# Batched matrix square roots in lanes: far sets in 29 rounds instead of 27, with reads back from DRAM, statistics loads and input loads moved in their queues

## The chip, the cores and the metric

The kernel runs on one core of a Trainium2 chip. A core has engines with an instruction queue each, which run in order: TensorE (PE; its weight loads are shown as PEld), VectorE (DVE), ScalarE (ACT), GpSimd (POOL) and SyncE (SP), which here only issues DMAs. They wait for each other through semaphores. DMAs are issued from SyncE's and ScalarE's queues and carried by 16 DMA engines. The metric is the device time of one execution in microseconds, lower is better. Before the change it is 2986.16 us, the median of three runs (2984.56 to 2987.19).

## The reference

The input `x` has 32 batches of 32 channels of 128x128 matrices, in float32. Two layers add to it:

```python
def _L0_conv_ref(A):                       # 1024 matrices, 128x128
    normA = jnp.sqrt(jnp.sum(A2 * A2, axis=(1, 2)))
    Y = A2 / normA[:, None, None]; Z = I
    for _ in range(5):                     # Newton-Schulz, matrix square root
        T = 0.5 * (3.0 * I - jnp.matmul(Z, Y))
        Y = jnp.matmul(Y, T)
        Z = jnp.matmul(T, Z)
    return Y * jnp.sqrt(normA)[:, None, None]

x = x + _L0_conv_ref(_gn(x))               # _gn: group norm, 16 groups of 2 channels
x = x + _L1_conv_ref(_gn(x), weights1, weights2)
```

`_L1_conv_ref` takes the real part of a 2-D Fourier transform, multiplies 32x32 low modes (two corners) by real weights over the channels, and takes the real part of the inverse transform.

## The kernel before, in words

**Sets.** Four channels of one batch are a set, so there are 32 x 8 = 256 sets. The square root of a set is a fixed chain of products on TensorE: each product is four matmuls of 128x128, one for each channel, into one PSUM bank. Between two products VectorE or ScalarE takes the result out of PSUM, scaled and added to something. The generator `newton` (line 462) is the chain of one set; at each `yield` it hands over to the next set. `rest` stands for two yields.

**Lanes and rounds.** The main loop (lines 1115 to 1154) has nine lanes. In a round every lane that holds a set takes one step, up to the next `yield`. A set in a lane therefore advances by one step a round, and between two of its steps lie those of the other lanes. All engines' orders are exactly the order in which the steps issue their instructions (`keep_in_program_order`, line 88); no scheduler moves them. A new set starts when a lane is free and `due` is reached, which grows by `FAR` or `NEAR` rounds for each set (line 42).

**Near and far sets.** Both need a matrix `m` and its transpose `mb`. A near set (batch 0 and batches 19 to 31, 112 sets) transposes on TensorE (`near_quartic`, line 407). A far set (batches 1 to 18, 144 sets) transposes through DRAM: VectorE transposes 32x32 blocks out of PSUM (`turned`), a DMA writes them to DRAM (`away`, tile `turn`), and a second DMA reads them back in another order (`back`, tiles `w` and `mb`). There are three such round trips in a far set: one `w` in each of two `far_quartic` calls (line 442), and one `mb` in `newton` (line 481). The `far_quartic` of the second call takes `v` (a tile named `r`) that GpSimd makes from `mb` just before (line 486). In a far set 27 steps lie between start and end, and one starts every 27/9 = 3 rounds.

**Round-trip positions, before.** In `far_quartic` the way out follows the first product; the way back is issued two rounds later, and the product that uses `w` three rounds after that. `mb` goes back two rounds after its way out; its use by GpSimd follows four rounds later, in the same round as the next product.

**Inputs.** `fetch` (line 366) loads `b` and `xt` of a set, the latter transposed, three sets ahead of the lane's start: far sets on SyncE's queue, near sets on ScalarE's. `staged` (line 375) normalises them on ScalarE and GpSimd. `prep` (line 222) computes the group statistics of two batches at a time from a third copy `xs`, loaded on ScalarE's queue three steps ahead of the two `bn_stats` on VectorE that read it; all of the first loads are issued in its first step.

**After the square root.** `settle` (line 521) writes the sum to DRAM (`mid`), folds it on GpSimd for the Fourier transform and takes statistics on VectorE. `wide_products`, `small_products`, `last_products` and `inverse` (lines 670 to 1029) do the second layer; they run beside the near sets of batches 19 to 31, in steps that the main loop hands out by the round number. `weights` (line 848) loads weights of the last group into tiles that are free by then.

**Buffers.** Tiles come in rings. `rooms` (line 308) gives for each name the size of its ring and of a second part that exists until the end of the first 158 sets. DRAM tiles `turn` have a ring of 12. DMAs use eight completion semaphores in turn, so one is issued only when the one eight before it has landed.

Of the kernel before, what the change touches and what calls it, by code (L numbers as in the profile page):

```python
# [38 lines left out]
C = 32  # L39
G = 16  # L40
LANES, LESS = 9, 5
FAR, NEAR = 27 / 9, 25 / 5
GROUPS = (20, 7, 3, 2)


# [48 lines left out]
def conv_preact_kernel(  # L94
# [49 lines left out]
        od.append(dram.tile(shape, F32, name=f"od{i}", tag=f"od{i}"))  # L144
    where = [(i, b) for i, n in enumerate(GROUPS) for b in range(n)]

    stp = ctx.enter_context(tc.tile_pool(name="stp", bufs=4))
    up = ctx.enter_context(tc.tile_pool(name="up", bufs=1))
    sp = ctx.enter_context(tc.tile_pool(name="sp", bufs=1))
    small = ctx.enter_context(tc.tile_pool(name="small", bufs=1))  # L150
# [71 lines left out]
    def prep(bs, made):  # L222

        n = len(bs)
        nc_, ng = n * C, n * G
        first_b = bs[0]
        st = small.tile([P, ng, 6], F32, tag="a_st", name=f"a_st{first_b}", bufs=2)
        tiles = []
        parts = [(b, i) for b in bs for i in range(C // 4)]

        ahead = 3 if first_b else 8

        def load(k):
            b, i = parts[k]
            if first_b or i < 4:
                t = stp.tile([P, 2, 2 * P], F32, tag="xs", name=f"xs{b}_{i}")
            else:
                t = four("turn", True).rearrange("p (j c) x -> p j (c x)", j=2)
            src = xs_in[b, :, 2 * i : 2 * i + 2].rearrange("p g h c -> p g (h c)")
            kept(nc.scalar.dma_start(out=t, in_=src))  # L240
            tiles.append(t)

        for k in range(ahead):
            load(k)
        yield
        for k in range(len(parts)):
            for j in range(2):
                nc.vector.bn_stats(st[:, 2 * k + j, :], tiles[k][:, j, :])
            yield
            if k + ahead < len(parts):  # L250
                load(k + ahead)
        ms = small.tile([P, ng], F32, tag="a_ms", name=f"a_ms{first_b}")
        nm, d = yield from moments(st, ms, "a")
        yield from pause
        pq = bank()[:, 0, 0:nc_]
        nc.tensor.matmul(pq, avg_mean, d.rearrange("p g c -> p (g c)"), start=True, stop=True)
        if not first_b:
            warm(5)

        v = small.tile([P, nc_ + ng], F32, tag="a_v", name=f"a_v{first_b}")  # L260
        nc.vector.tensor_scalar_mul(v[:, 0:nc_], pq, -512 / (P * P))
        yield
        vg = small.tile([P, ng], F32, tag="a_vg", name=f"a_vg{first_b}")
        nc.vector.tensor_reduce(
            vg, v[:, 0:nc_].rearrange("p (g c) -> p g c", c=2), AX.X, ALU.add
        )
        nc.vector.tensor_scalar(v[:, nc_:], vg, 0.5, EPS, ALU.mult, ALU.add)
        yield
        s = small.tile([P, nc_ + ng], F32, tag="a_r_s", name=f"a_r_s{first_b}", bufs=2)
        yield from root(v, nc_ + ng, s)  # L270
        iv = small.tile([P, nc_ + ng], F32, tag="a_inv", name=f"a_inv{first_b}")
        nc.vector.reciprocal(iv, s)
        yield

        sc = small.tile([P, nc_], F32, tag="a_sc", name=f"a_sc{first_b}", bufs=2)
        nc.vector.tensor_scalar_mul(sc, iv[:, 0:nc_], MS / P)
        off = small.tile([P, ng, 2], F32, tag="a_off", name=f"a_off{first_b}", bufs=2)
        nc.vector.tensor_tensor(
            off,
            sc.rearrange("p (g c) -> p g c", c=2),  # L280
            nm[:, :, None].to_broadcast([P, ng, 2]),
            ALU.mult,
        )
        off = off.rearrange("p g c -> p (g c)")
        sn = small.tile([P, nc_], F32, tag="a_t_s", name=f"a_t_s{first_b}", bufs=3)
        for k, b in enumerate(bs):
            g, c = slice(k * G, k * G + G), slice(k * C, k * C + C)
            made[b] = (nm[:, g], sc[:, c], off[:, c], sn[:, c])
        yield
        nn = small.tile([P, ng, 2], F32, tag="a_d", name=f"a_n{first_b}")  # L290
        nc.vector.tensor_tensor(
            nn,
            s[:, 0:nc_].rearrange("p (g c) -> p g c", c=2),
            iv[:, nc_:, None].to_broadcast([P, ng, 2]),
            ALU.mult,
        )
        nn = nn.rearrange("p g c -> p (g c)")
        for far in sorted({is_far(b) for b in bs}):
            of = [k for k, b in enumerate(bs) if is_far(b) == far]
            c = slice(of[0] * C, of[-1] * C + C)  # L300
            f = EYE_Q * QS if far else EYE * QF
            nc.vector.tensor_scalar_mul(nn[:, c], nn[:, c], P * (1.5 / f) ** 2)
        yield
        yield from root(nn, nc_, sn)
        yield


    rooms = dict(b=(4, 6), xt=(10, 5), x=(3, 2), r=(4, 0), v=(3, 2), w=(3, 2), q=(4, 2))
    rooms.update(my=(4, 3), mb=(2, 4), t=(3, 2), y4=(2, 2), turn=(0, 4))
    turns = dict.fromkeys(rooms, 0)  # L310

# [28 lines left out]
    def minus(eye, m, t):  # L340

        nc.gpsimd.tensor_tensor(t, eye, m, ALU.subtract)
        return t
# [13 lines left out]
    def is_far(b):  # L357
        return 0 < b < FIRST
# [5 lines left out]
    raw = {}  # L364

    def fetch(b, g):
        queue = nc.sync if is_far(b) else nc.scalar
        xt, t = four("xt", has_more(b, g)), four("b", has_more(b, g))
        kept(queue.dma_start(out=t, in_=x[b, :, 4 * g : 4 * g + 4, :]))
        kept(queue.dma_start(out=xt, in_=xt_in[b, :, 4 * g : 4 * g + 4, :]))  # L370
        raw[b, g] = xt, t
# [35 lines left out]
    def near_quartic(m, mb, more):  # L407


        v = plus(m, -QA * MS, products(mb, m), "v", more)  # L410
        yield
        r = four("r", more)
        nc.gpsimd.tensor_tensor(r, mb, eye, ALU.add)
        yield
        w = plus(transposed(v), 1.0, r, "w", more)
        yield from rest
        q = plus(products(v, w), QF / (16 * MS**4), eye, "q", more)
        yield from rest
        return q
# [22 lines left out]
    def far_quartic(m, mb, v, f, later, more):  # L442

        ps = products(m, mb)
        held = away(turned(ps, more))
        if later:
            yield
        nc.vector.scalar_tensor_tensor(v, ps, 1 / (9 * MS), v, ALU.mult, ALU.add)
        if not later:
            yield  # L450
        minus(eye_q, m, m)
        yield
        w = back(held, "w", more)
        yield
        yield from rest
        q = plus(products(v, by_rows(w)), 9 / (39 * MS**2 * f**2), m, "q", more)
        yield from rest
        return q
# [3 lines left out]
    def newton(g, sn, xt, m, mb, v, far, more):  # L462
# [13 lines left out]
        if far:  # L476
            held = away(turned(ps, more))
            yield
            nc.scalar.mul(m, ps, MS / qf)
            yield  # L480
            mb = back(held, "mb", more)
            yield from rest
            yield from rest
            v = four("r", more)
            form = "p c (a j) -> p c a j"
            minus(eye_p.rearrange(form, a=4), by_rows(mb), v.rearrange(form, a=4))
            q = yield from far_quartic(m, by_rows(mb), v, TURNED, True, more)
            w, y4 = four("t", more), four("y4", more)
            nc.scalar.mul(w, products(q, by_rows(mb)), 1 / (MS * qf * TURNED))
            ps = products(q, y)  # L490
            for j in range(4):
                c = 4 * g + j
                nc.scalar.mul(y4[:, j, :], ps[:, j, :], sn[:, c : c + 1])
        else:
            nc.scalar.mul(m, ps, MS / qf)
            yield from rest
            mb = taken(transposed(m), "mb", more)
            yield from rest
            q = yield from near_quartic(m, mb, more)
            both = [bank().rearrange("p (j k) x -> p j k x", k=2) for _ in range(2)]  # L500
            for j in range(4):
                nc.tensor.matmul(both[j // 2][:, j % 2], q[:, j], my[:, j], start=True, stop=True)
            w, y4 = four("t", more), four("y4", more)
            for h in range(2):
                nc.scalar.mul(w[:, 2 * h : 2 * h + 2, :], both[h][:, :, 1, :], 1 / (MS * qf))
            for j in range(4):
                c = 4 * g + j
                nc.scalar.mul(y4[:, j, :], both[j // 2][:, j % 2, 0, :], sn[:, c : c + 1])
# [339 lines left out]
    def weights():  # L848


        kinds = [("b", 2)] * 3 + [("x", 2), ("b", 4), ("x", 4), ("x", 10)]
        kinds += [("my", 11)] * 2 + [("r", 12)] * 3 + [("mb", 15)] * 2 + [("v", 15)] * 2
        kinds += [("w", 16)] * 2 + [("my", 16), ("r", 17), ("v", 18)] + [("q", 19)] * 3
        first = B * C // 4 - 10
        spare = []
        for half in range(4, 2 * KK):
# [367 lines left out]
```

## Time and profile before

| what | value |
|---|---|
| median of three runs | 2986.16 us |
| profiled execution | 2981.79 us |
| its span, first to last instruction | 2980.0 us |
| TensorE busy (matmul) | 2849.7 us |
| VectorE busy | 2285.7 us |
| ScalarE busy | 1541.3 us |
| GpSimd busy | 1988.4 us |
| mean granted TensorE clock | 0.988 |
| bytes moved by DMA | 711.90 MB |

The page lists busy time, shares over time, DMA queues, the chain of work that ended last and the costliest groups of instructions. Views of the trace show more: who waited for whom (the engine and the tile it writes, the releaser, us in total, times, longest), the busy time of each engine in chosen stretches, the instructions of one tile, and instructions in order of time, where the number in brackets is the idle time before one and what ended it. A name such as `w<-turn` says what an instruction writes and reads; all instructions carry line 88, the recording helper's, so tiles and not lines tell them apart. A float32 matmul shows as two passes, so one product of four matmuls shows as eight.

### The profile page before, as it was taken

Reading aid. Unit: us, or ns where it says so; the run is one execution under the profiler, and the core shown is the slowest. Engines: PE = TensorE matmul, PEld = TensorE weight load, DVE = VectorE, ACT = ScalarE, POOL = GpSimd, SP = SyncE. Lnnn points to the kernel's source line nnn. Section 1 sums busy time; section 2 is a strip of 40 time slices with the busy share of each in tenths; the row PEclk is TensorE's granted clock in tenths of the full one; section 3 lists DMA queues with packets and bytes.
Section 4 is the critical chain, followed back from the end, with each engine's and each line's share of the span. In section 5 each row is a group of like instructions: output and inputs, shape, how many; then the busy total and the mean of one; then the engine's idle time right before and its main releaser. Section 6 shows DMA issues by size and latency. Waiting matters only on the chain.

```text
span 2980.0 us, 73661 instructions
## 1 busy us (share of the span) xinstructions
PE 2849.7 (96%) x27688; PEld 2663.8 (89%) x27688; DVE 2285.7 (77%) x4407; ACT 1541.3 (52%) x3899; POOL 1988.4 (67%) x2308
## 2 busy tenths in 40 slices
PE   7999999999999999999999999999999999999995
PEld 7899999999999899999999888888888899888983
DVE  7878898889788888888876545886876876777665
ACT  4555555555555555555544445545555544655452
POOL 4667767777777767767755534777777763678452
PEclk9999999999999999999999999999999999999997
DMA  5688889888888889898943566867877737666567
GB/s 177 199 280 272 253 267 281 275 266 282 269 275 257 283 253 294 253 291 255 303 139 104 157 203 208 284 231 242 281 242 248 261 124 226 209 230 218 186 211 268
DMA packets 566897, 711.90 MB, mean 239 GB/s; under 512 B 94736, under 2 KB 329232, under 8 KB 566544
## 3 DMA queue, kind: packets, MB, share of 16 engines
q1 hardware_dynamic: 494400, 574.26, 59.9%
q10 hardware_dynamic: 72144, 132.94, 13.7%
q8 instruction: 221, 3.62, 0.5%
q14 instruction: 132, 1.08, 0.1%
HBM read 440.17 MB, written 266.86 MB: 237 GB/s over the span
## 4 chain that ended last, share of the span: by engine, by line
PE 72%; DMA 12%; DVE 9%; issue 2%; POOL 2%; ACT 1%; SPq 1%; ACTq 0%; DVEq 0%; POOLq 0%
PE ps L88 72%; DMA xs<-in_xs 3%; DMA w<-turn 3%; DVE yt L88 1%; DVE turn L88 1%; DMA turn<-turn 1%; DVE b_d L88 1%; DMA yt<-mid 1%; DMA ob<-od 1%; DVE a_st L88 1%; DVE root L88 1%; DVE q L88 1%; DVE b_st L88 1%; SPq L88 1%; DVE v L88 1%
## 5 line engine op out<-in xcount | busy, mean ns | idle before, releaser
L88 POOL TENSOR_TENSOR fold<-xt 128x256 f32<-128x256 f32 x512 | 364.1, 734 | 308.4 <-DVE xt L88 274.2
L88 ACT ACTIVATE b<-b,a_off,a_sc 128x128 f32<-128x128 f32 x1024 | 467.2, 492 | 127.2 <-issue 27.9
L88 ACT ACTIVATE my<-ps 128x512 f32<-128x512 f32 x512 | 302.4, 602 | 410.4 <-PE ps L88 278.0
L88 PE MATMUL ps<-my,q 128*128 128x128 f32 (+1 forms) x2944 | 475.9, 309 | 6.5 <-ACT my L88 6.4
L88 POOL TENSOR_TENSOR yt<-yt,d 128x512 f32<-128x512 f32 x244 | 306.6, 1283 | 212.3 <-ACT d L88 192.8
L88 PEld LDWEIGHTS ps<-my,q 128*128 128x128 f32 x2944 | 411.9, 191 | 35.4 <-ACT my L88 7.6
L88 PE MATMUL ps<-w,v 128*128 128x128 f32 x2944 | 399.2, 279 | 26.1 <-DMA w<-turn 11.9
L88 POOL TENSOR_TENSOR v<-eye_v,b 128x512 f32<-128x512 f32 x144 | 184.0, 1278 | 352.2 <-ACT b L88 316.2
L88 ACT ACTIVATE t<-ps 128x256 f32<-128x256 f32 (+1 forms) x368 | 171.1, 467 | 462.8 <-PE ps L88 447.2
L88 PEld LDWEIGHTS ps<-w,v 128*128 128x128 f32 x2944 | 362.2, 193 | 41.7 <-issue 10.5
L88 POOL TENSOR_SCALAR x<-xt,a_nm,a_sc 128x128 f32<-128x128 f32 x736 | 323.7, 456 | 15.3 <-DVE a_sc L88 15.0
L88 DVE STREAM_TRANSPOSE turn<-ps 128x512 f32<-128x512 f32 x432 | 295.4, 698 | 45.3 <-PE ps L88 36.9
L88 ACT ACTIVATE y<-ps,a_t_s 128x128 f32<-128x128 f32 x1024 | 292.2, 372 | 42.9 <-PE ps L88 42.7
L88 PE MATMUL ps<-q,t 128*128 128x128 f32 x2048 | 273.4, 277 | 1.3 <-DVE r L88 1.3
L88 PEld LDWEIGHTS ps<-q,t 128*128 128x128 f32 x2048 | 249.0, 192 | 4.2 <-DVE r L88 1.5
L88 DVE BATCH_NORM_STATS2 a_st<-xs 128x6 f32<-128x256 f32 x504 | 184.9, 409 | 77.9 <-DMA xs<-in_xs 77.5
L88 DVE SCALAR_TENSOR_TENSOR w<-ps,r 128x512 f32<-128x512 f32 x224 | 152.9, 683 | 108.7 <-PE ps L88 75.3
L88 DVE SCALAR_TENSOR_TENSOR q<-ps,eye 128x512 f32<-128x512 f32 x224 | 153.3, 684 | 94.2 <-PE ps L88 90.1
L88 DVE TENSOR_TENSOR xt<-ps,xt 128x512 f32<-128x512 f32 x256 | 174.4, 681 | 50.6 <-PE ps L88 48.2
L88 POOL TENSOR_TENSOR r<-mb,eye 128x512 f32<-128x512 f32 x112 | 143.1, 1278 | 86.3 <-ACT mb L88 86.3
L88 DVE TENSOR_TENSOR yt<-ps,yt 128x512 f32<-128x512 f32 x256 | 163.0, 681 | 46.5 <-PE ps L88 40.9
L88 DVE BATCH_NORM_STATS2 b_st<-xt 128x6 f32<-128x256 f32 x512 | 188.0, 407 | 0.5
(147 smaller groups left out, 6296.5 us busy)
## 6 DMA issues: line engine op xcount, KB each, us to landing
turn<-turn SPq DMA_DIRECT2D x432, 256.0 KB
w<-turn SPq DMA_DIRECT2D x288, 256.0 KB
mid<-xt SPq DMA_DIRECT2D x256, 256.0 KB
yt<-mid SPq DMA_DIRECT2D x128, 512.0 KB
xs<-in_xs ACTq DMA_DIRECT2D x252, 256.0 KB
out<-yt SPq DMA_DIRECT2D x115, 512.0 KB
b<-in_x SPq DMA_DIRECT2D x144, 256.0 KB
xt<-in_xt SPq DMA_DIRECT2D x144, 256.0 KB
```

The lines of the kernel that those rows point to most:

```text
L88: return self.tc.keep_in_program_order(issue(*args, **kw))
```

## The change

- `FAR` becomes 29/9, so a far set starts every 3.22 rounds on average, and its steps become 29: one more in each of the two `far_quartic` calls, between the way out and the way back of `w`.
- In `newton` the two rests before the second `v` become one rest, one yield, the GpSimd operation, and one yield: it is issued a round sooner in the set than its next product.
- In `near_quartic` GpSimd's `r` is issued in the step of the square (the product `mb` by `m`), not one later.
- `b` and `xt` of all batches but the first are loaded on SyncE's queue: 104 near sets change queue.
- `xs` is loaded five steps ahead, with six buffers instead of four.
- The rings change to make room: `xt` (10, 5) to (10, 4), `r` 4 to 3, `q` (4, 2) to (3, 3); `weights` takes other tiles accordingly.

```diff
-FAR, NEAR = 27 / 9, 25 / 5
+FAR, NEAR = 29 / 9, 25 / 5
...
-    stp = ctx.enter_context(tc.tile_pool(name="stp", bufs=4))
+    stp = ctx.enter_context(tc.tile_pool(name="stp", bufs=6))
...
-        ahead = 3 if first_b else 8
+        ahead = 5 if first_b else 8
...
-    rooms = dict(b=(4, 6), xt=(10, 5), x=(3, 2), r=(4, 0), v=(3, 2), w=(3, 2), q=(4, 2))
+    rooms = dict(b=(4, 6), xt=(10, 4), x=(3, 2), r=(3, 0), v=(3, 2), w=(3, 2), q=(3, 3))
...
     def fetch(b, g):
-        queue = nc.sync if is_far(b) else nc.scalar
+        queue = nc.sync if b else nc.scalar
...
     def near_quartic(m, mb, more):
-        v = plus(m, -QA * MS, products(mb, m), "v", more)
-        yield
         r = four("r", more)
         nc.gpsimd.tensor_tensor(r, mb, eye, ALU.add)
+        v = plus(m, -QA * MS, products(mb, m), "v", more)
+        yield
         yield
         w = plus(transposed(v), 1.0, r, "w", more)
...
     def far_quartic(m, mb, v, f, later, more):
         minus(eye_q, m, m)
-        yield
+        yield from rest
         w = back(held, "w", more)
         yield
         yield from rest
...
     def newton(g, sn, xt, m, mb, v, far, more):
             mb = back(held, "mb", more)
             yield from rest
-            yield from rest
+            yield
             v = four("r", more)
             form = "p c (a j) -> p c a j"
             minus(eye_p.rearrange(form, a=4), by_rows(mb), v.rearrange(form, a=4))
+            yield
             q = yield from far_quartic(m, by_rows(mb), v, TURNED, True, more)
...
     def weights():
-        kinds += [("my", 11)] * 2 + [("r", 12)] * 3 + [("mb", 15)] * 2 + [("v", 15)] * 2
-        kinds += [("w", 16)] * 2 + [("my", 16), ("r", 17), ("v", 18)] + [("q", 19)] * 3
+        kinds += [("my", 11)] * 2 + [("r", 12)] * 2 + [("mb", 15)] * 2 + [("v", 15)] * 2
+        kinds += [("w", 16)] * 2 + [("my", 16), ("r", 17), ("v", 18), ("y4", 19)] + [("q", 19)] * 2 + [("q", 21)]
```

More of the change, by code (lines that the diff above doesn't have):

```diff
@@ L407, in near_quartic @@
     def near_quartic(m, mb, more):
+        r = four("r", more)
+        nc.gpsimd.tensor_tensor(r, mb, eye, ALU.add)
         v = plus(m, -QA * MS, products(mb, m), "v", more)
         yield
-        r = four("r", more)
-        nc.gpsimd.tensor_tensor(r, mb, eye, ALU.add)
         yield
```

## The prediction

> **What bounds the kernel now.** I read the page first, then the stretches, then who waited for whom (TensorE, then SyncE and VectorE), and last the order of time around single stalls.
>
> ```profile
> PE 2849.7 (96%) x27688; PEld 2663.8 (89%) x27688; DVE 2285.7 (77%) x4407; ACT 1541.3 (52%) x3899; POOL 1988.4 (67%) x2308
> ```
> ```profile
> 0.00:200.00 200.00, 178.06 (x1442) 167.32 (x1443) 150.68 (x325) 98.75 (x250) 117.15 (x150) 0.98 0.64 205
> 200.00:1500.00 1300.00, 1269.96 (x11491) 1226.56 (x11491) 1104.39 (x2170) 699.01 (x1793) 954.06 (x1059) 1.00 0.87 273
> ...
> 1700.00:2900.00 1200.00, 1160.44 (x12479) 1054.39 (x12470) 853.05 (x1569) 627.73 (x1569) 782.32 (x932) 0.99 0.68 225
> 2900.00:2980.00 80.00, 46.00 (x508) 30.22 (x506) 42.36 (x74) 23.61 (x55) 27.57 (x24) 0.76 0.77 271
> ```
> Columns: stretch, length, busy TensorE matmul, weight load, VectorE, ScalarE, GpSimd, granted clock, DMA share, GB/s. The far sets fill 200 to 1500 us: TensorE lacks 30.0 of 1300 us there at full clock, and 39.6 us in the late near stretch. TensorE bounds both; the change removes no matmul, so only these 70 us, and some of the 22 us before 200 us, can be won. The end (after 2900) is not touched.
>
> ```profile
> PE ps L88 <- DMA w<-turn: 20.0, 20, 3.2
> PE ps L88 <- DVE a_ms L88: 11.2, 1, 11.2
> PE ps L88 <- DVE w L88: 10.5, 10, 2.8
> ...
> PE ps L88 <- ACT my L88: 6.8, 4, 2.9
> ...
> PE ps L88 <- DVE r L88: 3.2, 3, 1.3
> ```
> The largest named wait is for `w` coming back from DRAM: 20 times, 20.0 us, of which 17.3 us lie between 200 and 1500.
>
> ```profile
> SPq L88 <- DMA turn<-turn: 319.4, 228, 5.4
> SPq L88 <- DVE turn L88: 214.5, 172, 6.3
> ```
> ```profile
> 214.88 2.19 SPq L88 DMA_DIRECT2D turn<-turn  x3
> 220.21 0.92 SPq L88 DMA_DIRECT2D w<-turn  x2
> 221.29 0.40 SPq L88 DMA_DIRECT2D mb<-turn  x1
> ```
> SyncE's waits from 200 to 1500, and its order of time: with a set every 3 rounds the three ways out fall into one round and the three ways back two rounds later, next to each other in the queue. SyncE stands until its own way out has landed (319 us in all), then issues the backs in one burst.
>
> ```profile
> 1153.60 1.06 PE L88 MATMUL ps<-q,t 128*128 128x128 f32 x8
> 1155.34 1.13 PE L88 MATMUL ps<-w,v 128*128 128x128 f32 x8 [0.69 <-DMA w<-turn]
> ```
> A product is eight passes and starts 0.89 us after the one before it (1152.70, 1153.60). This one waited for a `w` issued at 1149.08, which took 6.1 us.
>
> ```profile
> DVE a_st L88 <- DMA xs<-in_xs: 77.5, 47, 6.7
> ...
> DVE w L88 <- POOL r L88: 19.7, 15, 2.9
> ...
> DVE r L88 <- POOL r L88: 13.3, 12, 3.0
> ...
> DVE w L88 <- POOL x L88: 10.9, 7, 2.4
> ```
> ```profile
> 2274.36 6.41 ACTq L88 DMA_DIRECT2D xs<-in_xs  x3
> 2280.82 0.60 ACT L88 ACTIVATE my<-ps 128x512 f32<-128x512 f32 x1 [7.63 <-DMA out<-yt]
> ```
> VectorE, in order, stands for statistics inputs and for GpSimd. ScalarE stands inside a burst of three `xs` issues (an issue waits for the DMA eight before it, on either queue); TensorE lost 2.4 us behind this one and 2.9 us behind one at 2059.
>
> **The change part by part.** The sum is made against the profiled execution, 2981.8 us (span 2980.0 and 1.8 around it); the median of the runs is 2986.2, 4.4 us more. About 6 us (0.2%) is what a measurement can tell from no change.
>
> *29 rounds, `w` back three rounds behind.* From way out to consuming product there are 6 rounds instead of 5. The rounds get shorter, because nine lanes do the same work in 29 rounds: the second square's `w` products start at 138.8 us first and 1545.1 last, so a far set takes 1406.3 / 143 = 9.8 us (3 rounds of 3.28 us before, 3.22 of 3.05 after), and 16.4 us becomes 18.3. From way back to product there remain 3 rounds, 9.8 us before, 9.1 after. The back is moved on SyncE past two or three issues of 0.33 to 0.45 us, some of them other sets' ways out, which wait for VectorE. In the instruction order I counted, for the first square, the products between the last one that any way out ahead of the back needs and the one that uses `w`: median 12.0 us before, 8.9 after; lowest tenth 8.9, then 7.1; least 7.1, then 6.2. For the second square the median stays (12.5, 12.6). Against it stands what the way takes. From 200 to 1500 a `w` lands 2.6 to 9.2 us after its issue, median 4.4. Where the count was 7.5 us or less (12 backs) it landed 6.4 us after the product in the median, nine of ten within 7.6, and 4 of 12 were late, for 1.7 us together: 0.14 us a back. With counts of 9.2 to 12 us, mostly backs that stood for their own way out, 0.27 us a back was lost. After the change that standing goes, and I take the short row, to which the new counts are nearest: 144 first squares by 0.06 to 0.14, 9 to 20 us, of which 9, since three quarters of the counts are above 7.9; second squares 1. Instead of 20.0 that is 10. In the filling of the lanes, before 200 us, the counts fall to 3.6 and rounds are shorter: 2 more. Net -8; ends -20 (no wait left) and +20 (0.28 us a back on all 144, twice today's).
>
> *Shorter rounds for all else.* Two rounds, 6.6 us, become 6.1. Results of VectorE and ScalarE with under 4 us of products as cover: 119 before and 137 after in the far stretch. TensorE waits for these two engines in the far stretch for about 11 us; in proportion +2, and I take +3 with ends 0 and +8. Ways out spread over the rounds also spread VectorE's work, which speaks for less.
>
> *`xs` five ahead.* The load of a tile runs five steps ahead of its use, not three: 15 us instead of 9.8, against the 5.2 us that a load takes in the median. VectorE's 77.5 us of waits should nearly go. They are a fifth of its idle time in the far stretch (42.6 of 195.6 us), and TensorE waits for VectorE about 7.3 us there: -2, ends -5 and 0. The price: every block of statistics now begins with five issues in a row on ScalarE. Three take 1.3 us unhindered (0.43 each) and up to 6.41. Fifteen such bursts with two more issues and two more DMAs waited for: I take 3 to 4 us a burst, about the cover of a ScalarE result, so +4 in all; ends -3 (the two dear bursts fall otherwise) and +32 (2.5 us each, less the 5.3 paid now).
>
> *`r` in front of its square, the second `v` a round sooner.* GpSimd does the same 112x2 and 144 operations of 1.28 us, earlier, past the four staging operations of 0.46 us. Nothing new is waited for: its inputs are two or more rounds old, except the second `v`, whose `mb` has three rounds instead of four (9 us, against 5.0 us in the median from issue to landing). `r` then has two rounds, not one, and the 19.7 and 13.3 us of VectorE waits should go, most of the 10.9 too. TensorE waits for `w` and `r` of VectorE 10.5 and 3.2 us: I take half, -6; ends -12 and +2 (GpSimd standing for `mb`, which holds folds and unfolds).
>
> *`b`, `xt` on SyncE.* 104 near sets move 208 issues of 0.34 to 0.44 us, some 80 us, off ScalarE, which TensorE waits for some 8 us in the late stretch, most of it behind `xs`: -1.5; ends -5 and +5. On SyncE they wait for a free `b` (four late) and `xt` (ten), with `mid`, `yt`, `out` and the weights behind them; in the order 19 us of products or more lie between issue and use, and TensorE waits for weights only 7.4 us now. If that cover went, it would show there.
>
> The rule "Issuing engines are not separate DMA queues" of the Trainium skill (DMA: Bandwidth & Descriptors) says that DMAs from any engine share the same 16 DMA engines, so that choosing the issuer saves only issue time. It speaks against this edit: by it the term would be 0 and the forecast 1.5 us later; the trace shows ScalarE standing at issues for far longer than the issue itself (6.41 us for three), which the rule's "usually small" leaves out.
>
> *Buffers.* `xt` 14 not 15, `r` three, `q` three and three, other late weight tiles: 0. An `xt` has 6.4 rounds (19 us) from the end of its set to its reuse instead of 9, a `mid` store lands in 4.3; an `r` lives 7 of 9.7 rounds (three sets). Without that cover SyncE or GpSimd would stand.
>
> Sum: -8 +3 -2 +4 -6 -1.5 = -10.5: 2971.3 for a profiled execution, 2976 for the median.
>
> **The rivals.**
> *The way back itself is now too short (slower).* Place: the first square's `w`. If it lands as in the row of 7.5 to 9.2 us (8 backs, median 8.2, 1.7 us lost), 144 lose 0.21 each, 31 us; at 0.28, 40. Against today's 20 that is +11 to +20, and with the rest (-2.5) 2995 to 3004. It decides as soon as half the backs come later than 8.9 us after the product. For it: DMA share 0.87. Against: that row holds backs that stood for their own way out.
> *Five issues hold ScalarE.* At 6 us each, as the two dear bursts: +32 instead of +4, sum +17.5: 3004. For it: 6.41 us for three. Against: in far blocks three took 1.3 to 3.8.
> *Hidden anyway.* TensorE at 98% only exchanges one wait for another: `w` -3, `r` -2, the rest +2: within 6 us, 2983.
>
> **How the numbers follow.** Faster as summed 0.52 (2962 to 2980 its own range), hidden 0.18, the way back 0.16, the bursts 0.14. Predicted is the likeliest, 2976. The range goes down to 2955 (`w` and `r` near their good ends) and up to 3000, into both slower rivals. Faster 0.52, same 0.18, slower 0.30.
>
> **What would show it.** Right: TensorE's wait for `w` near 10 us; SyncE's wait for `turn` far below 319; VectorE's for `xs` below 25; for GpSimd's `r` below 10. Wrong: TensorE's wait for `w` above 30; issues of five `xs` over 5 us with `my` or `t` late behind them; new waits for `diag` or `yt`.

## The result and the profile after

The changed kernel takes 3004.12 us (median of 7 runs, 2999.65 to 3010.59); the kernel before took 2985.2 beside it (7 runs, 2972.97 to 2998.74). The ratio is 1.0075, 95% interval 1.0053 to 1.0097: slower by three quarters of a per cent. 2976 had been forecast, between 2955 and 3000. The profiled execution took 3004.12 us, with a span of 3002.3 (before 2981.79 and 2980.0).

First the page's busy times, then the same stretches as before (columns: stretch, length, busy matmul, weight load, VectorE, ScalarE, GpSimd, granted clock, DMA share, GB/s):

```profile
PE 2853.5 (95%) x27688; PEld 2669.3 (89%) x27688; DVE 2275.8 (76%) x4407; ACT 1531.2 (51%) x3899; POOL 1988.7 (66%) x2308
```
```profile
0.00:200.00 200.00, 177.41 (x1444) 166.64 (x1444) 152.69 (x333) 101.04 (x256) 122.00 (x155) 0.98 0.68 215
200.00:1500.00 1300.00, 1238.12 (x11129) 1194.49 (x11131) 1065.69 (x2090) 677.92 (x1737) 921.21 (x1019) 0.99 0.83 262
...
1700.00:2900.00 1200.00, 1179.11 (x12780) 1077.29 (x12781) 859.82 (x1610) 628.19 (x1594) 793.38 (x954) 0.99 0.70 226
```

TensorE ran the same number of instructions, at a mean granted clock of 0.985 (0.988 before). In the far stretch TensorE now lacks 61.9 of 1300 us (30.0 before), in the late near stretch 20.9 of 1200 (39.6 before). So the change lost in one place and won in another. A cut by events says the same. The last product of `w` and `r` in the second square of a far set ends at 1545.5 us before and at 1599.8 after, 54.3 later. From there to the last product of `q` and `t`, which belongs to the last near set, it is 1357.9 us before and 1326.4 after, 31.5 less. The rest is 76.6 and 76.1. Below these two are called the far part's end and the near part.

Who waited for whom (total, times, longest; over the whole span), TensorE and then VectorE:

```profile
PE ps L88 <- DMA w<-turn: 52.7, 35, 3.5
...
PE ps L88 <- ACT my L88: 7.9, 7, 2.3
...
PE ps L88 <- DVE w L88: 4.7, 6, 1.7
```
```profile
DVE a_st L88 <- DMA xs<-in_xs: 22.7, 9, 4.8
...
DVE w L88 <- POOL x L88: 1.6, 2, 1.0
...
DVE w L88 <- POOL r L88: 1.4, 1, 1.4
```

VectorE's waits for `xs` and for GpSimd's `r` went as foreseen (77.5 to 22.7, 19.7 to 1.4). But TensorE's wait for `w` is 52.7 us instead of 20.0: 35 waits instead of 20, and longer ones. The growth of this one line, 32.7 us, exceeds the whole loss. SyncE, which issues the ways back, from 200 to 1500 us:

```profile
SPq L88 <- DVE turn L88: 277.3, 166, 6.6
SPq L88 <- DMA turn<-turn: 249.9, 115, 4.7
```

It stands less for ways out that have not landed (319.4 before), and more for VectorE's transposes (214.5 before), that is, at ways out that cannot be issued yet, with the backs of other sets behind them in its queue. One late back in order of time (start, length, what is issued), on SyncE and on TensorE:

```profile
861.86 0.32 SPq L88 DMA_DIRECT2D mid<-xt  x1
865.12 0.37 SPq L88 DMA_DIRECT2D mb<-turn  x1
865.59 0.46 SPq L88 DMA_DIRECT2D turn<-turn  x1
866.13 0.38 SPq L88 DMA_DIRECT2D w<-turn  x1
866.57 0.70 SPq L88 DMA_DIRECT2D b<-in_x  x1
```
```profile
866.85 1.06 PE L88 MATMUL ps<-w,r 128*128 128x128 f32 x8
867.74 1.06 PE L88 MATMUL ps<-q,t 128*128 128x128 f32 x8
872.28 1.13 PE L88 MATMUL ps<-w,v 128*128 128x128 f32 x8 [3.48 <-DMA w<-turn]
873.25 1.85 PE L88 MATMUL ps<-mb,my 128*128 128x128 f32 x8
874.89 1.91 PE L88 MATMUL ps<-q,my 128*128 128x128 f32 x8
```

SyncE issues nothing from 862.2 to 865.1. Then come an `mb`, a way out and the `w`, which takes 6.1 us to land. When it is issued only two products are left as cover, and TensorE stands for 3.48 us.

The stall costs more than its own length. The two products behind it take 1.85 and 1.91 us instead of 1.06, because the granted clock (third number from the end) is halved just then:

```profile
873.40:876.80 3.40, 3.40 (x19) 3.40 (x18) 2.62 (x6) 0.00 (x0) 1.27 (x1) 0.51 0.85 278
```

Such stretches of 3.4 us at half the clock, some of them two on end, come with 7 of the 11 waits of TensorE over 2.5 us between 200 and 2800 us. Between 200 us and the far part's end there are seven, and one before the change. Up to the far part's end all waits of TensorE add up to 92.6 us (51.7 before), and the half clock is worth an estimated 15.3 us (5.1 before; half of each stretch's length): together 51.1 of the 54.3 us lost. In the near part it is 22.4 us of waits (43.7 before) and 8.5 of half clock (10.2), 23.0 of the 31.5 won.

### The profile page after: what moved, and what is told of

Its sections match the earlier page's. It is cut to its first block, busy times and chain, and to the rows that moved or that the text cites. A ratio compares the mean times of both kernels' runs of the same rounds, so it can differ in the third digit from the quotient of the medians.

```text
span 3002.3 us, 73720 instructions
## 1 busy us (share of the span) xinstructions
PE 2853.5 (95%) x27688; PEld 2669.3 (89%) x27688; DVE 2275.8 (76%) x4407; ACT 1531.2 (51%) x3899; POOL 1988.7 (66%) x2308
## 4 chain that ended last, share of the span: by engine, by line
PE 75%; DMA 11%; DVE 7%; issue 3%; POOL 2%; ACT 1%; SPq 1%; ACTq 0%; DVEq 0%; POOLq 0%
PE ps L88 75%; DMA w<-turn 5%; DMA xs<-in_xs 1%; DMA turn<-turn 1%; DVE turn L88 1%; DVE yt L88 1%; DVE q L88 1%; DVE a_st L88 1%; DMA out<-yt 1%; DVE v L88 1%; SPq L88 1%; DMA mid<-xt 1%; POOL x L88 1%; DVE b_d L88 0%; POOL fold L88 0%
## 5 line engine op out<-in xcount | busy, mean ns | idle before, releaser
L88 ACT ACTIVATE b<-b,a_off,a_sc 128x128 f32<-128x128 f32 x1024 | 460.9, 493 | 60.2 <-DMA xs<-in_xs 15.9
L88 DVE STREAM_TRANSPOSE turn<-ps 128x512 f32<-128x512 f32 x432 | 301.4, 703 | 55.6 <-PE ps L88 44.8
L88 POOL TENSOR_SCALAR x<-xt,a_nm,a_sc 128x128 f32<-128x128 f32 x736 | 321.9, 451 | 15.3 <-DVE a_sc L88 15.3
L88 POOL TENSOR_TENSOR my<-eye_q,my 128x512 f32<-128x512 f32 x144 | 183.8, 1276 | 99.9 <-PE ps L88 89.0
L88 DVE BATCH_NORM_STATS2 a_st<-xs 128x6 f32<-128x256 f32 x504 | 184.5, 408 | 22.7 <-DMA xs<-in_xs 22.7
L88 POOL TENSOR_TENSOR r<-eye_p,mb 128x512 f32<-128x512 f32 x144 | 183.7, 1275 | 27.1 <-DMA mb<-turn 17.2
```

What stands on the lines that cost most here:

```text
L88: return self.tc.keep_in_program_order(issue(*args, **kw))
```

## The experiments

Each kernel was compared with the kernel before on its own chip, whose median lay between 2985 and 2991 us. Ratios are given with their 95% intervals; one per cent is 30 us. At the start there were three theories. A: the way back of `w` now comes too late, and this is the far part's loss. B: bursts of five `xs` issues hold ScalarE. C: starts every 3.22 rounds, an uneven rhythm, mix the rounds. e1 to e5 set them against each other, e4 and e6 to e8 follow B, e9, e10 and e14 to e16 look for what the near sets won, e11 to e13, e17 and e18 for the right place of the way back and the best version.

### Which part loses

**e1.** The changed kernel with the far steps of before:

```diff
-FAR, NEAR = 29 / 9, 25 / 5
+FAR, NEAR = 27 / 9, 25 / 5
...
-        yield from rest
+        yield
         w = back(held, "w", more)
...
             yield from rest
-            yield
+            yield from rest
             v = four("r", more)
...
-            yield
```

> The changed kernel with its far part undone: FAR 27/9, way back of w two rounds behind its way out, second v as before; all else as changed. Theory A (the loss is the far part's: the way back of w, now in a queue among other ways out, comes too late): the far loss of some 40 us goes, what the near parts won stays; 2965 to 2972, TensorE's wait for w near 20 us. Theory B (the bursts of five xs issues hold ScalarE and cost the time): the loss stays, 2995 to 3005.

2985.95 us, ratio 1.0004 (0.9986 to 1.0022), between the two theories' ranges. The far steps carry the loss, but what is left wins nothing either. TensorE's wait for `w` is 13.3 us up to 1540; one wait of 7.5 us for ScalarE's `t` and three of 5.5 us in all for its `z` are new.

**e2.** The reverse: the kernel before with the far part of the change alone (29/9, the back three rounds behind, the second `v` sooner).

> The kernel before with the far part alone: 29 rounds, way back three rounds behind, second v a round sooner. Theory A: 3015 to 3030, more than the whole change, since nothing of the near parts is won; TensorE's wait for w 45 to 60 us. Theory B: within 10 us of before, 2975 to 2995.

3017.08 us, ratio 1.0096 (1.0070 to 1.0123), and the `w` wait up to 1540 us is somewhat longer than in the whole change (52.7):

```profile
PE ps L88 <- DMA w<-turn: 58.4, 35, 4.2
```

The far part's end is at 1601.1 us: 55.6 later than before, where it was 54.3 with the whole change.

**e3.** The changed kernel with the extra round on the other side of the way back: two rounds behind the way out as before, four ahead of the product.

```diff
-        yield from rest
-        w = back(held, "w", more)
         yield
+        w = back(held, "w", more)
+        yield from rest
         yield from rest
```

> The changed kernel with the added round moved to the other side of the way back of w: two rounds behind the way out, four ahead of the product; still 29 rounds and the same starts. In the instruction order the products between the last one that a way out ahead needs and the one that uses w rise for the first square from 8.9 to 14.4 us in the median, the least from 6.2 to 10.7. Theory A: TensorE's wait for w falls under 15 us and the time to 2955 to 2972. Theory C (the uneven starts, every 3.22 rounds, mix the rounds of the nine lanes and so cost the time, wherever the way back stands): 2995 to 3005 still.

2967.43 us, ratio 0.9931 (0.9905 to 0.9957). The issue of one line, moved by one round, turns +0.75% into -0.69%. Number and rhythm of the rounds are those of the changed kernel, so theory C alone can't be the cause. Its waits of TensorE up to 1540 us:

```profile
PE ps L88 <- ACT my L88: 14.7, 5, 5.3
PE ps L88 <- DMA w<-turn: 11.9, 8, 4.6
```

With `w` out of the way, ScalarE comes first. What theory B says can be seen at one place in its order of time and TensorE's:

```profile
1440.88 6.41 ACTq L88 DMA_DIRECT2D xs<-in_xs  x5
1447.33 0.60 ACT L88 ACTIVATE my<-ps 128x512 f32<-128x512 f32 x1 [6.61 <-DMA xs<-in_xs]
```
```profile
1447.98 2.07 PE L88 MATMUL ps<-q,my 128*128 128x128 f32 x8 [5.30 <-ACT my L88]
```

**e5.** The changed kernel with 27 steps in a set, but started every 29/9 rounds (e1 without its first hunk).

> The changed kernel with far sets of 27 steps as before, started every 29/9 rounds. The count for the first square is 10.7 us in the median, least 6.2; second square 10.7, least 8.0. Theory C: about the changed kernel's time, 2995 to 3010. Theory A: between: more counts under 9 us than before in both squares, wait for w 30 to 50 us, 2980 to 3000.

3017.38 us, ratio 1.0096 (1.0070 to 1.0122). Not what either theory expected. Lanes now stand empty for two rounds in 29. The `w` wait is 32.4 us, between the two others, and the near part takes 1368.5 us, 42 more than in the changed kernel, though none of its steps differs. TensorE waits longer there (51.2 us in all against 22.4, for VectorE, ScalarE, DMAs and GpSimd alike) and has more half clock (an estimated 17.1 us against 8.5). Why the waits are longer is not settled, nor is it shown that an uneven rhythm costs nothing.

### The bursts of xs

**e4.** The changed kernel with `xs` three ahead again (`bufs=4`, `ahead = 3`).

> The changed kernel with xs three steps ahead and four buffers, as before the change. Theory B (bursts of five xs issues hold ScalarE 6 to 9 us each) as part of the loss: VectorE waits about 40 us more for xs, but the bursts get short again; 2990 to 3000 instead of 3004, and TensorE's waits for ACT my and ACT t fall. Theory A alone (the way back of w carries all the loss): 3002 to 3008, with the w wait still 45 to 55 us.

3003.32 us, ratio 1.0057 (1.0037 to 1.0076). The intervals overlap: here the bursts cost at most a little. The `w` wait is 58.2 us, the wait for ScalarE's `my` 1.0: TensorE only exchanged one for the other.

**e6.** e3 with the same edit.

> The changed kernel with the extra round behind the way back of w, and with xs three ahead. If the bursts are what is left of the loss there (TensorE waited 14.7 us for ACT my and 5.4 for ACT t in the version with five ahead, 2967 us): 2950 to 2962. If the standing of VectorE for xs costs as much as the bursts: 2964 to 2972. If it costs more: 2975 or above.

2952.73 us, ratio 0.9894 (0.9866 to 0.9922), 0.37% below e3, although VectorE waits 58.9 us for `xs` from 200 to 1500. The two intervals still overlap a little.

**e7.** e3 with five ahead, but the first five loads spread over three steps:

```diff
         for k in range(ahead):
             load(k)
+            if first_b and k % 2 == 0 and k < ahead - 1:
+                yield
         yield
```

> The changed kernel with the extra round behind the way back of w, and with the first five xs loads issued one, two and two in three steps instead of five in one. If the length of one burst in ScalarE's order is what costs: 2952 to 2963, with VectorE's xs wait still below 15 us. If ScalarE stands at these issues however they are grouped (each waits for the DMA eight before it): 2965 to 2970.

2952.06 us, ratio 0.9890 (0.9861 to 0.9919). Five ahead without the burst is as fast as three ahead (e6), so the distance costs nothing to be seen. TensorE's wait for `my` up to 1540 us falls from 14.7 us in e3 to 4.2 in e6 and here to:

```profile
PE ps L88 <- ACT my L88: 4.9, 5, 2.8
```

**e8.** e1 with `xs` three ahead, so that `r` in front, the loads on SyncE and the rings are left.

> 27 rounds and the far steps as before the change, with xs three ahead: only r in front of its square, b and xt on SyncE, and the rings are left of the change. If these win what the prediction gave them and only the bursts hid it in the version with five ahead (2986): 2975 to 2981. If they win nothing: 2983 to 2988. If five ahead had been the better of the two: above 2988.

2969.23 us, ratio 0.9943 (0.9923 to 0.9963), 0.61% below e1. So the bursts cost 18 us (e1 to e8, clear of the noise) and some 11 us (e3 to e6, at its edge) where `w` is not late, and 5 or nothing where it is. With e4 the price of the far steps follows at three ahead: 0.9943 to 1.0057, +1.14% or 34 us; and with e6 that of one round: 1.0057 to 0.9894, 49 us.

### The parts of the near sets

**e9.** The kernel before with `r` in front of its square, and nothing else.

> The kernel before, with nothing changed but r in front of its square in the near sets. The near parts together (r, loads on SyncE, rings) gave 18 us with xs three ahead. If r carries them: 2968 to 2976, and VectorE's wait for GpSimd's r near 0. By the prediction's step (half of the 13.7 us that TensorE waited for w and r, some of it far): 2981 to 2985. If r only takes an idle VectorE's wait away: 2985 to 2990.

2995.93 us, ratio 1.0022 (1.0005 to 1.0038): slower by about 7 us. GpSimd's waits after 1500 us, in the kernel before and in this one:

```profile
POOL r L88 <- ACT mb L88: 72.4, 25, 9.6
```
```profile
POOL r L88 <- ACT mb L88: 128.7, 43, 9.8
```

VectorE's `w` hardly waits for `r` any more (1.1 us), but GpSimd, in order, stands for `mb` with its other work behind it.

**e10.** The kernel before with `b` and `xt` of near sets on SyncE's queue, and nothing else (the one line of `fetch`).

> The kernel before, with nothing changed but b and xt of the near sets loaded on SyncE's queue. If this carries the 18 us of the near parts: 2968 to 2976. By the prediction's step (1.5 us): 2984 to 2987. If SyncE's waits for free xt and b hold mid, yt and the weights back: 2990 or above, with new waits for diag or plain.

2962.31 us, ratio 0.9935 (0.9912 to 0.9957). This one line, priced at 1.5 us, wins about 19 by the ratio and 26 by the medians; the near part is 25.7 us shorter, of which 17.3 are fewer waits of TensorE and an estimated 8.5 less half clock. TensorE's waits from 1600 to 2900 us in the kernel before, of which the first two do not occur in e10 and the last is 0.7 us there:

```profile
PE ps L88 <- DMA diag<-in_wk: 7.4, 4, 2.9
...
PE ps L88 <- ACT my L88: 6.4, 3, 2.9
...
PE ps L88 <- DMA plain<-xs: 3.3, 2, 1.9
```

And SyncE's in the same stretch, before and in e10:

```profile
SPq L88 <- DMA yt<-mid: 93.4, 42, 6.0
```
```profile
SPq L88 <- DMA yt<-mid: 55.1, 44, 3.7
```

SyncE took over 186 issues in this stretch and yet waited less for its own earlier DMAs, and the weights (`diag`, `plain`) came in time. That the one made the other is argued, not tested by itself.

**e14 and e15.** The changed kernel with one of these two parts undone: `r` behind its square again (e14), near loads on ScalarE again (e15).

> The changed kernel (3004 us) with r of the near sets behind its square again. If r's cost, 7 to 8 us when done alone, is part of the changed kernel's loss: 2995 to 2998. If r pays or costs nothing beside the other parts: 3002 to 3010.

> The changed kernel (3004 us) with b and xt of the near sets loaded on ScalarE's queue again. If the 25 us that the loads on SyncE won when done alone are also won inside the changed kernel: 3022 to 3034, all of it in the near stretch. If the other parts had already won them: 3004 to 3010.

3001.32 us, ratio 1.0056 (1.0033 to 1.0078), and 3030.53, ratio 1.0149 (1.0125 to 1.0172). The loads' 22 us are won inside the changed kernel too; its near part grows from 1326.4 to 1347.3 us without them. For `r` the 6 us agree with e9, but the interval overlaps that of the changed kernel.

**e16.** e10 with `xs` on SyncE as well, so that ScalarE issues nothing after the start.

> The kernel before with b, xt and also xs of all batches but the first loaded on SyncE's queue, so that ScalarE issues no DMA after the start. With b and xt alone it was 2962 us. If the gain of the loads comes from ScalarE being free of issues: 2945 to 2958. If it came only from an order in SyncE's queue that suits b and xt: 2960 to 2966. If xs in SyncE's queue has to stand behind ways out and comes late for VectorE: 2970 or above, with VectorE's wait for xs above 80 us.

2960.42 us, ratio 0.9915 (0.9895 to 0.9936), not to be told from e10. VectorE waits 75.0 us for `xs` from 200 to 1500 us, and that costs nothing to be seen. SyncE's wait for `yt<-mid` falls to 32.4 us. A ScalarE free of all issues had been expected at 2945 to 2958; nothing of that is seen beyond e10.

### Where the way back belongs, and the best version

**e11.** e7 with the way back one round behind the way out, five ahead of the product.

```diff
-        yield
         w = back(held, "w", more)
+        yield
         yield from rest
         yield from rest
```

> The version with the way back two rounds behind the way out and the xs loads spread (2952 us), with the way back one round behind instead, five ahead of the product. If only the room ahead of the product counts: 2946 to 2953. If a back so soon makes SyncE stand for its own way out again and holds what is queued behind it (the 319 us of waits for turn came from that): 2955 to 2975, and SyncE's wait for DMA turn above 300 us.

3094.25 us, ratio 1.0364 (1.0338 to 1.0390), far beyond what was expected. Up to 1540 us TensorE waits, and from 200 to 1500 SyncE:

```profile
PE ps L88 <- DMA mb<-turn: 94.6, 40, 6.2
PE ps L88 <- DVE a_ms L88: 11.2, 1, 11.2
PE ps L88 <- DMA w<-turn: 10.7, 12, 1.6
```
```profile
SPq L88 <- DMA turn<-turn: 565.7, 249, 6.1
```

`w` itself is in time. But SyncE stands 566 us for its ways out (396.2 in e7), and the `mb` backs, which share its queue, come late.

**e12.** e7 with the second `v` in the round of its product, as before the change.

> The version with the way back two rounds behind the way out and the xs loads spread (2952 us), with the second v of far sets made in the round of its product again, as before the change. If the second v made sooner is worth what the prediction's step gave it (a part of 6 us): 2953 to 2958, with VectorE waiting for GpSimd's r again. If it is worth nothing: 2950 to 2953. If an earlier place had only done harm (GpSimd standing for mb): below 2950.

2960.24 us, ratio 0.9908 (0.9882 to 0.9935), against 0.9890 of e7. The second `v` made sooner is worth less than these runs can tell.

**e13.** e7 with `r` of the near sets behind its square again.

> The version with the way back two rounds behind the way out and the xs loads spread (2952 us), with r of the near sets behind its square again, as before the change. r alone cost the kernel before 7 to 8 us. If it costs the same here: 2943 to 2947. If its cost was hidden by other parts of the change: 2950 to 2954.

2938.90 us, ratio 0.9855 (0.9829 to 0.9881), 10 us less than e7 by the ratios, though the intervals overlap. VectorE's wait in question, after 1600 us, is back and larger than it ever was, and costs TensorE nothing that shows:

```profile
DVE w L88 <- POOL r L88: 51.1, 27, 3.4
```

**e17.** e13 with the `xs` loads on SyncE too (the edit of e16).

> The best version so far (back two rounds behind, xs spread, r as before: 2939 us) with the xs loads of all batches but the first on SyncE's queue too. In the far stretch TensorE waited 7.8 us for ScalarE's my there; if that comes from the xs issues and nothing takes its place: 2931 to 2936. If xs in SyncE's queue adds to what stands in front of the backs of w: 2942 or above, with the w wait above 22 us. If the two cancel: 2937 to 2941.

2935.39 us (2934.31 to 2937.81), ratio 0.9816 (0.9793 to 0.9840): the best version, 1.8% faster than the kernel before. That `xs` on SyncE adds to e13 is not shown, for the intervals overlap. Its stretches:

```profile
200.00:1500.00 1300.00, 1275.37 (x11524) 1232.92 (x11523) 1112.65 (x2173) 696.55 (x1788) 954.49 (x1059) 1.00 0.87 272
...
1700.00:2900.00 1200.00, 1171.58 (x12737) 1061.16 (x12736) 854.04 (x1607) 628.46 (x1593) 791.32 (x938) 0.99 0.72 234
```

TensorE lacks 24.6 and 28.4 us there, against 30.0 and 39.6 before the change. It reaches the end of the far part at 1542.5 us, and its near part takes 1316.8.

**e18.** e13 with 31 steps started every 31/9 rounds: the way back two rounds behind the way out, five ahead.

> The best version so far (2939 us) with one round more between the way back of w and its product: two behind the way out, five ahead of the product, 31 steps started every 31/9 rounds. If room ahead of the product is all that counts, the w wait falls below 10 us and the time to 2928 to 2936. If the version with one round behind and five ahead (3094 us) lost to the five ahead and not to the one behind, this one loses as well: above 2960, with TensorE waiting for mb. If shorter rounds only raise other waits: 2938 to 2950.

3008.39 us, ratio 1.0064 (1.0042 to 1.0086). TensorE's waits up to 1540 us:

```profile
PE ps L88 <- DMA mb<-turn: 21.7, 17, 3.1
...
PE ps L88 <- DVE t L88: 10.4, 6, 2.8
PE ps L88 <- DVE q L88: 6.9, 8, 3.0
...
PE ps L88 <- DMA w<-turn: 2.1, 2, 1.8
```

The wait for `w` is nearly gone, as expected of the room, and the time is 62 us longer than e13's by the ratios. In the far part, which ends 25 us later than e13's, TensorE waits for `mb` instead, which has the same rounds but shorter ones, and for `t` and `q` of VectorE. The near part is 52 us longer (1365.3 against 1313.8), with 53.8 us of TensorE's waits against 17.8 and more half clock (an estimated 23.9 us against none); as in e5, why is not settled. By its expectation a time above 2960 with TensorE waiting for `mb` speaks for the five ahead as the cause of e11's loss. The sizes speak for the one round behind as the larger part: the wait for `mb` is 21.7 us here and 94.6 there, and SyncE stands 314.3 us for its ways out and 565.7 there. But e18 also changes the number of rounds, so the two causes are not separated.

## Why the prediction was wrong

**29 rounds, the way back three rounds behind: forecast -8, measured +29 alone (e2), +34 with three ahead (e4 against e8).** This is the step that failed: TensorE's wait for `w` was to fall from 20 to 10 us, and it rose to 52.7. The mechanism had been seen and put among the rivals, "the way back itself is now too short", with 0.16 and 2995 to 3004 us, and its place, the first square's `w`, was right: from 200 to 1500 us TensorE's wait there went from 9.2 to 32.1 us, at the second square from 8.1 to 10.7. The step's price was wrong. The prediction took 0.06 to 0.14 us a back from a row of 12 backs and applied its low end to all 144 first squares, since most counts lay above that row. The 0.14 set the landing against the counted room; where the 0.06 comes from it does not say. Here are both squares' backs from 200 to 1500 us, by the same count, with the time that TensorE stood for them (backs, waits, us):

| products between, us | before | after | us a back, before and after |
|---|---|---|---|
| 7.5 or less | 12, 2, 1.0 | 30, 16, 22.4 | 0.08, 0.75 |
| 7.5 to 9.2 | 8, 1, 0.6 | 66, 10, 15.0 | 0.08, 0.23 |
| over 9.2 | 244, 16, 15.6 | 158, 4, 5.4 | 0.06, 0.03 |

The short row holds the first square alone, and it cost nine times what it had cost before. A `w` there landed 7.1 us after the product in the median, not 6.4, and 21 of 30 landed after their room, which is 7.1 us in the median. That these two rows count is what e3 shows: with the back a round sooner the least count is 10.7 us, and the wait is 11.9. A second cost stood nowhere in the sum: the half clock behind long stalls, an estimated 10 us more in the far part.

The prediction also held it against this rival that the short rows were backs that "stood for their own way out" and that this standing goes. It did: in the median a `w` back is issued 2.5 us after its own way out has landed, 0.07 before. But this bought nothing: the round was given to the way out, while the way back kept its three rounds, which became shorter, and now stands behind other sets' ways out. The extra round was useful (e3, e6, e7), on the other side of the issue.

**`xs` five ahead: forecast -2 and +4.** VectorE's wait went as said (22.7 us, below 25), and its gain can't be seen: e16 lives with 75.0 us of it in the far stretch alone. The prediction read TensorE's wait for VectorE in the far stretch as 7.3 us; the view gives 8.4, which changes nothing. The bursts were the dearer half. In the changed kernel they cost 5 us or less, near the forecast, only because TensorE stood for `w` anyway; without that, some 11 and 18 us. The rival "five issues hold ScalarE" had the mechanism, and 32 us was too much for it.

**`r` in front, second `v` sooner: forecast -6.** The wait of VectorE for GpSimd's `r` went (19.7 to 1.4 us), and the time did not: `r` alone is +7 us (e9), some +10 in e7 against e13 with overlapping intervals, the second `v` nothing that can be told (e12). The bad end of this term was +2, "GpSimd standing for `mb`". That is what happened, 72.4 to 128.7 us, on the near sets' `mb`. A wait of VectorE was read as TensorE's, though e13 shows 51.1 us of it at no cost that can be seen.

**`b` and `xt` on SyncE: forecast -1.5, measured -19 alone and -22 inside.** The largest gain of the change was its smallest term, and outside its ends (-5 and +5). The prediction looked only at ScalarE, 8 us of TensorE's waits in the late stretch. In the near part, from the far part's end to the last near set, TensorE's waits add up to 43.7 us before and 26.4 in e10: for ScalarE 8.3 and 1.8, for DMAs 11.8 and 2.4, for VectorE 21.7 and 21.9. The larger part of the waits saved was for SyncE's other DMAs, which the prediction had counted as a risk only, and a third of the gain was clock. The rule weighed there, "Issuing engines are not separate DMA queues" of the Trainium skill (DMA: Bandwidth & Descriptors), lets a choice of issuer save issue time only, and as the prediction read it the term would have been 0; e10 and e15 measure about 20 us. Why SyncE's earlier DMAs keep it waiting less when ScalarE issues fewer isn't shown. That an issue waits for the one eight before it, on either queue, fits; no run separates it from the order of the transfers.

**Shorter rounds: forecast +3; buffers: 0.** Neither was measured by itself. Shorter rounds don't stop e3, e6 and e7 from winning; at 31 steps (e18) `mb`, `t` and `q` come late. No wait of TensorE in the profile after points to a ring.

**The sum.** By ratios: loads -0.65% (e10), `r` +0.22% (e9), together -0.43, and -0.57 measured with the rings (e8); far steps +1.14 (e4 against e8), bursts +0.18 (the change against e4): the +0.75% of the whole change. Two errors of opposite sign, some -20 us on the loads and +40 on the far steps, partly hid each other in the near part's 31.5 us won and the far part's 54.3 lost. So it is in part luck that the time fell at the upper end of the rival's 2995 to 3004: the rival had priced the far steps at +11 to +20 us and the loads at -1.5.

## What to carry to other kernels

A round added to a round trip helps only on the side that is late: here the back was already issued when its own input had landed, and moving the issue a round later lost (e2), leaving it and using its result a round later won (e3), and moving it a round sooner lost most (e11). Price a tighter slack by the lower end of its distribution, and trust a row of twelve only for its sign. Long idle waits of VectorE, which is not the bound, cost nothing to be seen here (e13, e16). DMA issues taken off a computing engine can be worth more than that engine's own waits show (e10), or nothing (`xs` in e16), so each has to be measured.

## What the runs showed of the hardware that was not expected

- The DMA issue of one source line, 288 in an execution, moved by one round of some 3 us in an in-order queue, is worth 43 to 49 us of 3000 (e3 against the changed kernel, e6 against e4), at the same DMA bytes.
- With 7 of 11 stalls of TensorE over 2.5 us the granted clock fell to 0.5 for 3.4 us or more in the changed kernel's profile, and two products behind the one shown took 1.85 and 1.91 us instead of 1.06. In e10's near part a third of the 25.7 us won is clock, by estimate.
- Five DMA issues in a row took ScalarE 2.3 us unhindered and three 1.3; held up, a run of five took 7.2 us and one of three 8.1 in the changed kernel's profile, where the longest took 6.4 before. Spread over three steps the same five cost nothing that shows against three (e7, e6).
- A queue that was given 186 more DMA issues in 1300 us waited less for its own transfers, 55.1 instead of 93.4 us for `yt<-mid` (e10), and 32.4 with 80 more (e16).
